# A state-space vision block on one core: side work of the scans repriced, reordered and split into other lanes

## The chip, the cores and the metric

The kernel runs on one core of a Trainium2 chip. The metric is the device time of one execution in microseconds (us). The engines of the core are PE (TensorE), DVE (VectorE), ACT (ScalarE), POOL (GpSimd) and SP (SyncE), which issues the DMAs here. Each has a queue of its own, takes its instructions in order, and waits on semaphores for the others.

## What is computed

The input is 8 images of 96 channels and 64 x 64 positions. The first layer is a group norm, a layer norm, an input projection with a depthwise 3 x 3 convolution and SiLU, a selective scan in four directions, a gated layer norm, an output projection, and a convolutional branch with Gelu and channel attention. The second layer is linear attention without softmax and a feed-forward part in quantized numbers. Cut to its core:

```python
xi = silu(conv2d(xi, conv_w, conv_b, groups=D_INNER))        # D_INNER = 192
xs = concat([x_hwwh, flip(x_hwwh, -1)], 1)                   # K = 4 directions of length L = 4096
x_dbl = einsum('bkdl,kcd->bkcl', xs, x_proj_w)
dts, Bs, Cs = split(x_dbl, ...)                              # rank 6, and 16 + 16 states
delta = softplus(einsum('bkrl,kdr->bkdl', dts, dt_w) + dt_bias)
h = exp(delta * A) * h + (delta * u) * B                     # one step; 16 states a channel
y = einsum('bkdn,bkn->bkd', h, C) + Ds * u
...
y = layer_norm(sum of the four directions) * silu(z); x1 = inp * skip_scale + out_proj(y)
cb = conv2d(gelu(conv2d(layer_norm(x1))))                    # then gated by channel attention
```

All scans together are 8 images x 4 directions x 192 channels x 16 states, each of 4096 steps.

## The kernel before

**The scans.** The images are taken in four pairs, p = 0 to 3. For each p there are four directions k, for each k four pieces of the sequence of 1024 steps (ci), and for each piece three tiles of channels (T). That makes 192 jobs. A job has four groups, a group four units, and a unit is one tile of 128 rows (32 channels of 4 states) by 1024 steps. The loop at the end of `phase_b` goes over the units two at a time; such a step is called a pair here, so a group is two pairs, and there are 768 groups. For each pair:

- ACT makes two tiles da, the decays, `exp(A * delta)`, two units ahead (`decay`; da has four buffers);
- DVE multiplies pu by bm into pb twice and runs two scans into hc (`scan`);
- POOL keeps the last column (carry) and multiplies hc by cm.

Once a group PE spreads du over the states into the PSUM tile pu (`spread`, two matmuls of 512 columns). There is one pu, so the spread for the next group can begin only when DVE has done the multiplications of the second pair, and DVE needs it for the first pair of the next group. Once a group PE also adds up the states of the group before (`total`, 16 small matmuls into half of bank yp), and ACT copies that out (y).

**The side work.** All the rest runs between the scans: the norms, taps and projections of the pair of images that comes next (`before_scans`, with `norms` and `convs`), the gate and output projection of the pair before (`gate`), everything behind it (`rest`), transposes of the scan's sum (`columns`). Each of these is a Python generator, called a lane. `Slots` holds the lanes and is run twice for each pair, once ahead of the scan and once behind the decays and, in every second pair, behind spread and total. One run is a slot; `slots.at` counts them. Four slots are a group: 1 ahead of the first scan, 2 behind the decays that follow it, 3 ahead of the second scan, 0 behind the decays, spread and total. A job has 16 slots. In a slot each lane may issue instructions up to its next `yield`. A lane that needs a PSUM bank asks `take(pe, act)` with what the work costs PE and ACT, by a price written into the code; it gets the bank when it is free and both budgets are above zero. The budgets grow by RATE in each slot, up to CAP; `pay` books more. Slot 6 and 7 of a job belong to Softplus (`steps`), which uses both banks; a `take` marked long stays away from slots 4 to 7. `after(n, f)` puts off a call by n slots.

The order that results is binding: the wrapper `InOrder` ties each instruction of an engine to the one before it, which is why nearly every instruction of the profile carries its line, L245. Nothing moves at run time; a lane's instruction at the wrong place delays all that follow on its engine.

**What has to be there in time.** A job is prepared one job ahead. If its inputs are not made yet (`while (p, k % 2, c) not in there`), 16 slots are run without a scan.

**Buffers.** Lanes share tiles u0 to u15 (`unit(i)`), each with one buffer. `norms` uses two input tiles in turn, one for the transposed rows, one for the normalized rows, two for the layer norm. `convs` copies its three results raw and runs SiLU on all three together, since SiLU and Gelu need a table other than that of exp and ln: ACT loads it ahead, and `exps()` loads the first one again behind.

Of the kernel before, what the change touches and what calls it, by code (L numbers as in the profile page):

```python
# [25 lines left out]
R = 6  # L26
G = 32
CH = 1024
# [233 lines left out]
class Slots:  # L262
# [6 lines left out]
    RATE, CAP = (1.4, 1.6), (2.2, 2.2)  # L269

    def __init__(self, *banks):
        self.lanes, self.first, self.at, self.due = [], None, 0, {}
        self.banks, self.held, self.big = banks, set(), set()
        self.left = [0.0, 0.0]
# [4 lines left out]
    def take(self, pe, act, long=False):  # L279
        while True:  # L280
            i = 1 if self.at % 2 and not long else 0

            due = long and self.at % 16 in (4, 5, 6, 7)
            if i not in self.held and not due and min(self.left) > 0:
                self.held.add(i)
                self.pay(pe, act)
                return self.banks[i]
            yield
# [14 lines left out]
    def run(self):  # L303
        self.at += 1
        self.left = [min(v + r, c) for v, r, c in zip(self.left, self.RATE, self.CAP)]
        for f in self.due.pop(self.at, ()):
            f()
        if self.first is not None and next(self.first, self) is self:
            self.first = None
        turn = self.at % len(self.lanes) if self.lanes else 0  # L310
        for lane in self.lanes[turn:] + self.lanes[:turn]:
            if next(lane, self) is self:
                self.lanes.remove(lane)

    def idle(self):
        return not (self.lanes or self.first or self.due)


def wait(n):
    for _ in range(n):  # L320
        yield


class Slots:

    RATE, CAP = (1.4, 1.6), (2.2, 2.2)

    def __init__(self, *banks):
        self.lanes, self.first, self.at, self.due = [], None, 0, {}
        self.banks, self.held, self.big = banks, set(), set()
        self.left = [0.0, 0.0]

    def pay(self, *times):
        self.left = [v - t for v, t in zip(self.left, times)]

    def take(self, pe, act, long=False):
        while True:
            i = 1 if self.at % 2 and not long else 0

            due = long and self.at % 16 in (4, 5, 6, 7)
            if i not in self.held and not due and min(self.left) > 0:
                self.held.add(i)
                self.pay(pe, act)
                return self.banks[i]
            yield  # L350

    def take_big(self, *which):

        while self.big & set(which):
            yield
        self.big |= set(which)

    def give(self, bank):
        i = self.banks.index(bank)
        self.after(1, lambda: self.held.remove(i))  # L360

    def after(self, n, f):
        self.due.setdefault(self.at + n, []).append(f)

    def run(self):
        self.at += 1
        self.left = [min(v + r, c) for v, r, c in zip(self.left, self.RATE, self.CAP)]
        for f in self.due.pop(self.at, ()):
            f()
        if self.first is not None and next(self.first, self) is self:  # L370
            self.first = None
        turn = self.at % len(self.lanes) if self.lanes else 0
        for lane in self.lanes[turn:] + self.lanes[:turn]:
            if next(lane, self) is self:
                self.lanes.remove(lane)

    def idle(self):
        return not (self.lanes or self.first or self.due)


def wait(n):
    for _ in range(n):
        yield


class Slots:

    RATE, CAP = (1.5, 1.7), (2.2, 2.2)

    def __init__(self, *banks):
        self.lanes, self.first, self.at, self.due = [], None, 0, {}
        self.banks, self.held, self.big = banks, set(), set()
        self.left = [0.0, 0.0]

    def pay(self, *times):  # L400
        self.left = [v - t for v, t in zip(self.left, times)]

    def take(self, pe, act, long=False):
        while True:
            i = 1 if self.at % 2 and not long else 0

            due = long and self.at % 16 in (4, 5, 6, 7)
            if i not in self.held and not due and min(self.left) > 0:
                self.held.add(i)
                self.pay(pe, act)  # L410
                return self.banks[i]
            yield

    def take_big(self, *which):

        while self.big & set(which):
            yield
        self.big |= set(which)

    def give(self, bank):  # L420
        i = self.banks.index(bank)
        self.after(1, lambda: self.held.remove(i))

    def after(self, n, f):
        self.due.setdefault(self.at + n, []).append(f)

    def run(self):
        self.at += 1
        self.left = [min(v + r, c) for v, r, c in zip(self.left, self.RATE, self.CAP)]
        for f in self.due.pop(self.at, ()):  # L430
            f()
        if self.first is not None and next(self.first, self) is self:
            self.first = None
        turn = self.at % len(self.lanes) if self.lanes else 0
        for lane in self.lanes[turn:] + self.lanes[:turn]:
            if next(lane, self) is self:
                self.lanes.remove(lane)

    def idle(self):
        return not (self.lanes or self.first or self.due)  # L440
# [7 lines left out]
def phase_b(  # L448
# [8 lines left out]
    with ExitStack() as ctx:  # L457
# [106 lines left out]
        def steps(job):  # L564

            p, k, ci, c, T, at = where(job)
            if T == 0:
                sts[job // 3] = gp.tile([2 * R, CH], F32, name="st")
                r0 = 64 + R * (k // 2)
                for b in range(2):  # L570
                    nc.sync.dma_start(
                        sts[job // 3][R * b : R * b + R, :],
                        xd_d[k % 2][2 * p + b][r0 : r0 + R, at],
                    )
            dtw = gp.tile([2 * R, 128], F32, name="dtw")
            nc.sync.dma_start(dtw, a["dtw"][:, k, T, :])
# [7 lines left out]
            for i, hs in enumerate(halves):  # L584
# [4 lines left out]
                pe.matmul(bank, dtw, sts[job // 3][:, hs], start=True, stop=True)  # L589
# [80 lines left out]
        def gate(p, js, ready=lambda j: None):  # L670
# [12 lines left out]
            for n, at in enumerate(ats):  # L683
                then = ats[n + 1] if n + 1 < len(ats) else None
                xc, sq = [], []
                for T in range(3):
                    bank = yield from slots.take(1.0, 1.3)
# [20 lines left out]
                for T in (2, 0, 1):  # L708
                    bank = yield from slots.take(1.0, 2.1)
# [23 lines left out]
                for b in range(2):  # L733
                    bank = yield from slots.take(1.3, 0.6)
# [11 lines left out]
        def norm(u, v):  # L746

            bank = yield from slots.take(0.45, 1.2)
# [6 lines left out]
            bank = yield from slots.take(0.45, 2.0)  # L755
# [38 lines left out]
        def squeeze(s, u, pieces):  # L794
# [4 lines left out]
            for i in pieces:  # L799
# [4 lines left out]
                bank = yield from slots.take(0.8, 0.0, True)  # L804
                for tap in range(9):
# [9 lines left out]
                    if dx == 2 and tap < 8:  # L815
                        yield
                        slots.pay(0.8, 0.0)
# [18 lines left out]
        def rest(b, s):  # L836
# [29 lines left out]
            for j in range(8):  # L866
# [3 lines left out]
                bank = yield from slots.take(0.9, 0.0, True)  # L870
                for dx in range(3):
# [7 lines left out]
                    if dx == 1:  # L879
                        yield  # L880
                        slots.pay(0.45, 0.8)
# [78 lines left out]
            def fold(t, lhsT, rhs, m):  # L960
                bank = yield from slots.take(0.2, 0.3)
# [14 lines left out]
            for j in range(8):  # L976
                v = nx
                bank = yield from slots.take(0.9, 0.7)
# [20 lines left out]
                for i in range(3):  # L999
                    bank = yield from slots.take(0.2, 1.9)  # L1000
# [8 lines left out]
                bank = yield from slots.take(0.3, 1.3)  # L1009
# [91 lines left out]
        def before_scans(p):  # L1101
# [13 lines left out]
            def project(o, b, main, mix, rows, at, t=None):  # L1115
                half = b % 2
                bank = yield from slots.take(0.9, 0.6)
# [10 lines left out]
            def norms(b):  # L1128
                def u(i):
                    return unit((6 if at_once and b % 2 else 12) + i)  # L1130
# [4 lines left out]
                def fetch(j):  # L1135
                    t = u(j % 2)[:, 0 : 4 * C].rearrange("p (g c) -> p g c", c=C)
# [8 lines left out]
                for j in js:  # L1145
                    x = nxt
                    if j < 7:
                        nxt = fetch(j + 1)
# [11 lines left out]
                    yield  # L1160
                    bank = yield from slots.take(0.1, 2.5)
# [3 lines left out]
                    inp = u(3)[0:C, 0:512]  # L1165
                    for i, q in enumerate(quarters):
                        se.activation(
                            inp[:, q], xt[:, q], AF.Square, bias=ngm[:, i : i + 1],
# [9 lines left out]
                    yield from wait(3)  # L1178
                    for i, q in enumerate(quarters):
# [24 lines left out]
            def convs(b):  # L1204
# [5 lines left out]
                def u(i):  # L1210
                    return unit(3 * half + i if at_once else 12 + i)
# [13 lines left out]
                for j in js:  # L1225
# [7 lines left out]
                    for i, w in enumerate((wz, wmain, wmix)):  # L1233
                        bank = yield from slots.take(1.3 if i else 0.45, 0.0, i > 0)
                        taps = 1 if i == 0 else 9
                        for t in range(taps):
# [8 lines left out]
                            if t in (2, 5):  # L1245
                                yield
                                slots.pay(1.3, 0.0)
# [7 lines left out]
                    z, main, mix = raw  # L1255
                    slots.pay(0.0, 4.7)
# [12 lines left out]
                    t = gp.tile([128, 512], F32, name="turn", bufs=2) if at_once else None  # L1269
                    yield from project(0, b, main, mix, slice(0, 64), ats[j], t)  # L1270
# [25 lines left out]
            there_all = set()  # L1296
            if at_once:
                for half in range(2):
                    slots.lanes.append(convs(2 * p + half))
                    if p:  # L1300
                        slots.lanes.append(norms(2 * p + half))
                while len(there_all) < 2:
                    yield
            else:
                for half in range(2):
# [713 lines left out]
```

## Time and profile before

| | before |
|---|---|
| median of 3 runs | 11310.33 us (11296.98 to 11315.09) |
| profiled execution, its time | 11307.01 us |
| span of that execution | 11305.2 us |
| busy: PE, PEld | 8037.9, 3168.4 us |
| busy: DVE | 10538.6 us, 93% |
| busy: ACT | 6622.9 us, 59% |
| busy: POOL | 9032.5 us, 80% |
| mean granted PE clock | 0.813 |
| first multiplication by bm, last scan's end | 226.5, 10966 us |

Two costly groups of instructions and the busy shares over 40 slices of the span:

```profile
L245 DVE TENSOR_TENSOR_SCAN hc<-da,carry,pb 128x1024 f32<-128x1024 f32 x2304 | 5284.5, 2341 | 97.3 <-ACT da L245 84.7
L245 DVE TENSOR_TENSOR pb<-pu,bm 128x1024 f32<-128x1024 f32 x3072 | 3612.9, 1227 | 270.3 <-PE pu L245 244.6
...
DVE 4999899999998999999999999999999999999984
```

In a group's line come the engine, the operation, what it writes and reads, the shape and the count; then the busy time of all in us and the mean of one in ns; then the idle time of the engine just ahead of them, and what ended most of it. In the slices a 9 is 90% or more of a slice of 283 us.

### The profile page before, as it was taken

The page shows a single profiled execution, that of the slowest core. Times are in us where ns is not written, and L with a number is a line of the kernel's source. Part 1 is how long each engine was busy: PE and PEld are TensorE (multiplying, and loading weights), DVE is VectorE, ACT ScalarE, POOL GpSimd, SP SyncE. Part 2 cuts the span into 40 slices and gives each one's busy share as a digit, 9 for nine tenths or more (in the row PEclk, how much of TensorE's full clock was granted, in tenths as well). Part 3 has the DMA queues.
Part 4 walks back from the last instruction along what each step waited for, and adds up shares of the span by engine and source line. Part 5 has one row for each costly group of instructions (what it writes and reads, how often), then busy time and mean ns, then how long its engine had stood idle before and what let it go on. Part 6 is the DMA issues. An engine that isn't in the chain of part 4 may idle for free.

```text
span 11305.2 us, 127593 instructions
## 1 busy us (share of the span) xinstructions
PE 8037.9 (71%) x39452; PEld 3168.4 (28%) x39452; DVE 10538.6 (93%) x6651; ACT 6622.9 (59%) x9183; POOL 9032.5 (80%) x6649
## 2 busy tenths in 40 slices
PE   7856887555568868867667876677757676665778
PEld 3312332222223323323222332233222233222223
DVE  4999899999998999999999999999999999999984
ACT  2545665444465666657766666667645656774554
POOL 2787777877897887898888778988879889997870
PEclk8877888777778878878888888788878787777889
DMA  3455444543554566665454555655644555553551
GB/s 113 144 181 164 145 154 158 174 141 129 162 186 153 165 167 190 197 204 186 154 159 154 157 172 180 198 168 169 199 148 156 163 162 189 176 170 126 175 159 37
DMA packets 893945, 1832.98 MB, mean 162 GB/s; under 512 B 244797, under 2 KB 415742, under 8 KB 886222
## 3 DMA queue, kind: packets, MB, share of 16 engines
q1 hardware_dynamic: 893262, 1824.82, 51.5%
q8 instruction: 313, 5.13, 0.2%
q14 instruction: 370, 3.03, 0.1%
HBM read 1403.95 MB, written 420.42 MB: 161 GB/s over the span
## 4 chain that ended last, share of the span: by engine, by line
PE 39%; issue 24%; DVE 16%; POOL 8%; ACT 8%; DMA 4%; SPq 0%; DVEq 0%; POOLq 0%; ACTq 0%
PE yp L245 13%; PE pu L245 13%; PE pg L245 10%; DVE hc L245 9%; DVE pb L245 5%; POOL hc L245 5%; ACT u L245 3%; ACT da L245 3%; PE t L245 2%; ACT L245 1%; POOL u L245 1%; DMA bm<-xd 1%; POOL turn L245 1%; PE ps L188 1%; DMA cm<-xd 1%
## 5 line engine op out<-in xcount | busy, mean ns | idle before, releaser
L245 POOL TENSOR_TENSOR hc<-hc,cm 128x1024 f32<-128x1024 f32 x3072 | 7231.3, 2359 | 698.3 <-DVE hc L245 467.2
L245 DVE TENSOR_TENSOR_SCAN hc<-da,carry,pb 128x1024 f32<-128x1024 f32 x2304 | 5284.5, 2341 | 97.3 <-ACT da L245 84.7
L245 PE MATMUL pu<-du,c_sel 128*128 128x512 f32 x3072 | 2438.3, 939 | 2205.5 <-DVE pb L245 2201.9
L245 DVE TENSOR_TENSOR pb<-pu,bm 128x1024 f32<-128x1024 f32 x3072 | 3612.9, 1227 | 270.3 <-PE pu L245 244.6
L245 ACT ACTIVATE da<-dl,c_alog 128x1024 f32<-128x1024 f32 x3072 | 3363.0, 1142 | 143.7 <-DVE hc L245 121.8
L245 ACT COPY y<-yp 128x256 f32<-128x256 f32 x768 | 284.9, 371 | 2657.8 <-PE yp L245 2522.8
L245 PEld LDWEIGHTS pu<-du,c_sel 128*128 128x128 f32 x3072 | 799.3, 283 | 3469.7 <-DVE pb L245 2676.7
L245 DVE TENSOR_TENSOR_SCAN hc<-da,pb 128x1024 f32<-128x1024 f32 x768 | 1715.5, 2282 | 54.8 <-ACT da L245 53.5
L245 PE MATMUL yp<-hc,c_add 128*32 128x256 f32 x24576 | 1639.3, 411 | 39.3 <-ACT dls L245 34.4
L245 PEld LDWEIGHTS yp<-hc,c_add 128*32 128x32 f32 x24576 | 761.6, 119 | 1183.5 <-issue 608.0
L245 POOL COPY carry<-hc 128x1 f32<-128x1 f32 x2304 | 424.1, 184 | 806.3 <-DVE hc L245 771.1
L245 ACT ACT_TABLE_LOAD x570 | 731.3, 1283 | 27.0 <-DMA cb<-y 16.9
L245 POOL TENSOR_TENSOR u<-u,u 96x512 f32<-96x512 f32 (+1 forms) x426 | 538.1, 1269 | 115.1 <-ACT u L245 104.3
L245 POOL TENSOR_TENSOR du<-du,dls 128x1024 f32<-128x1024 f32 x192 | 453.4, 2361 | 158.3 <-ACT dls L245 156.5
L245 ACT COPY u<-pg 128x512 f32<-128x512 f32 (+5 forms) x384 | 212.8, 554 | 501.1 <-PE pg L245 490.2
L245 ACT COPY u<-yp 96x512 f32<-96x512 f32 (+5 forms) x336 | 179.9, 536 | 427.2 <-PE yp L245 409.1
L245 PE MATMUL pg<-ain,wmain 96*128 96x512 f32 x792 | 378.2, 622 | 30.3 <-ACT u L245 25.6
L245 PE MATMUL pg<-ain,wmix 96*128 96x512 f32 x792 | 370.9, 613 | 15.4 <-ACT u L245 15.0
L245 PE MATMUL yp<-prev,ident 128*128 128x256 f32 x768 | 308.1, 492 | 10.5 <-ACT dls L245 9.0
L245 PEld LDWEIGHTS yp<-prev,ident 128*128 128x128 f32 x768 | 211.6, 277 | 340.3 <-issue 272.5
L245 PE MATMUL yp<-u,c_centres 128*128 128x512 f32 (+3 forms) x622 | 284.2, 660 | 27.0 <-ACT u L245 15.2
L245 PE MATMUL pg<-st,dtw 12*128 12x512 f32 x384 | 223.9, 663 | 45.3 <-ACT u L245 26.7
(341 smaller groups left out, 7152.8 us busy)
## 6 DMA issues: line engine op xcount, KB each, us to landing
dl<-dl SPq DMA_DIRECT2D x768, 512.0 KB
bm<-xd SPq DMA_DIRECT2D x512, 512.0 KB
cm<-xd SPq DMA_DIRECT2D x512, 512.0 KB
du<-xi SPq DMA_DIRECT2D x192, 512.0 KB
dl<-dls SPq DMA_DIRECT2D x192, 512.0 KB
ya<-y SPq DMA_DIRECT2D x384, 128.0 KB
prev<-ya SPq DMA_DIRECT2D x384, 128.0 KB
xi<-u SPq DMA_DIRECT2D x152, 256.0 KB
```

Of the source, the lines that this page charges most:

```text
L188: nc.tensor.matmul(pc.rearrange("p (h w) -> p h w", w=W), w[:, t, :], pad[:, 8 * j + dy : 8 * j + dy + 8, dx : dx + W], start=(t == 0), st ...
L245: op(*args, **kw)
```

## The change

- `Slots` stood in the file three times, each hiding the one before it; one is left. Its refill goes from (1.5, 1.7) us a slot for PE and ACT to (1.7, 1.7), its cap from 2.2 to 2.4.
- Nearly all prices of PE are about doubled; some of ACT are lowered (that of ln and exp from 2.0 or 2.1 to 1.3).
- A long `take` names its length in slots and stays away from slot 6 of a job if it would reach it.
- SiLU waits for a slot 2 of a group (`slots.at % 4`), but not slot 6 of a job. The last taps ahead of Gelu, and Gelu, wait for an even slot.
- Lanes are in two lists. `before_scans`, `norms` and `convs` stand in `later`, which is served behind `lanes`, unless `behind()` says that fewer rows than one in 35 slots are done (for p of 2 and 3).
- For p of 2 and 3, norms of both images in turn are one lane and the taps of both are another, where there was one lane for all. The taps use the tiles u16 and up.
- `norms` has one input tile, fetched for the next row behind the transposes; it squares into another tile and normalizes in place. `project` behind the taps writes into the tile of z, raw[0].
- st and dtw hold the two halves of a piece in rows 0 to 11 and 32 to 43, in half the columns, with one load for each half; the two matmuls use these rows.

```diff
-    RATE, CAP = (1.5, 1.7), (2.2, 2.2)
+    RATE, CAP = (1.7, 1.7), (2.4, 2.4)
...
-            due = long and self.at % 16 in (4, 5, 6, 7)
+            due = self.at % 16 <= 6 < self.at % 16 + long
...
-        turn = self.at % len(self.lanes) if self.lanes else 0
-        for lane in self.lanes[turn:] + self.lanes[:turn]:
-            if next(lane, self) is self:
-                self.lanes.remove(lane)
+        order = [self.lanes, self.later]
+        for lanes in order[::-1] if self.behind() else order:
+            turn = self.at % len(lanes) if lanes else 0
+            for lane in lanes[turn:] + lanes[:turn]:
+                if next(lane, self) is self:
+                    lanes.remove(lane)
...
-                pe.matmul(bank, dtw, sts[job // 3][:, hs], start=True, stop=True)
+                rows = slice(32 * i, 32 * i + 2 * R)
+                pe.matmul(bank, dtw[rows, :], sts[job // 3][rows, :], start=True, stop=True)
...
-                    bank = yield from slots.take(1.0, 2.1)
+                    bank = yield from slots.take(1.8, 1.3)
                     minus_mean(bank, sq, T)
...
-            bank = yield from slots.take(0.45, 1.2)
+            bank = yield from slots.take(0.9, 1.2)
             pe.matmul(bank[0:C, :], centre, v, start=True, stop=True)
...
                     if dx == 2 and tap < 8:
                         yield
-                        slots.pay(0.8, 0.0)
+                        while tap == 5 and slots.at % 2:
+                            yield
+                        slots.pay(1.2, 0.0)
...
-                        bank = yield from slots.take(1.3 if i else 0.45, 0.0, i > 0)
+                        bank = yield from slots.take(2.6 if i else 0.9, 0.0, 3 if i else 0)
...
-                                slots.pay(1.3, 0.0)
+                                slots.pay(2.6, 0.0)
...
+                    while slots.at % 4 != 2 or slots.at % 16 == 6:
+                        yield
                     slots.pay(0.0, 4.7)
                     se.activation(main, main, AF.Silu, bias=convb[:, 0:1])
...
-                    t = gp.tile([128, 512], F32, name="turn", bufs=2) if at_once else None
-                    yield from project(0, b, main, mix, slice(0, 64), ats[j], t)
+                    yield from project(0, b, main, mix, slice(0, 64), ats[j], u(0)[:, 0:512])
...
-                for half in range(2):
-                    yield from norms(2 * p + half)
-                    yield from convs(2 * p + half)
+                begun = slots.at
+                slots.behind = lambda: slots.at - begun > 35 * len(rows_done)
+                def both(f):
+                    yield from f(2 * p)
+                    yield from f(2 * p + 1)
+                slots.later += [both(norms), both(convs)]
```

## The prediction

> **What bounds the kernel now.** First the slices of the page: DVE is at 9 tenths or more nearly everywhere. So I cut the span by the stages of the side work (stretches in us; then length, busy time and count of each engine, granted PE clock, DMA share, GB/s):
>
> ```profile
> core 0: us, PE busy (x) PEld busy (x) DVE busy (x) ACT busy (x) POOL busy (x), PEclk, DMA share, GB/s
> 1063.00:1917.00 854.00, 697.22 (x3030) 283.84 (x3033) 769.91 (x456) 537.07 (x883) 613.78 (x449) 0.86 0.48 150
> 1917.00:2980.00 1063.00, 572.06 (x3092) 223.74 (x3088) 1061.70 (x634) 455.31 (x491) 849.53 (x605) 0.73 0.45 147
> 2980.00:3982.00 1002.00, 740.23 (x3361) 275.76 (x3354) 916.20 (x544) 613.57 (x947) 855.07 (x657) 0.83 0.54 172
> 4364.00:5256.00 892.00, 693.63 (x3136) 271.05 (x3138) 834.59 (x500) 547.88 (x728) 788.23 (x633) 0.82 0.62 200
> 5713.00:7070.00 1357.00, 1046.91 (x5310) 404.38 (x5304) 1292.62 (x771) 885.95 (x1340) 1120.37 (x808) 0.84 0.55 165
> 7070.00:7983.00 913.00, 673.09 (x3179) 270.27 (x3171) 861.56 (x513) 618.94 (x872) 805.41 (x645) 0.81 0.56 182
> ```
>
> Where side work is thin (1917 to 2980) DVE idles 1.3 us of 1063: the scans alone set the pace, 6.7 us a pair, 13.47 us a group of two pairs. Where norms and taps run, DVE idles 84 (854 - 770), 86, 57, 64 and 51 us. Over the loop (227 to 10966) the same subtraction gives 411 us. That is all this change can win; the 227 us ahead of the loop and the 339 us behind it are untouched. The waits of DVE say who takes it:
>
> ```profile
> engine line waited for: us in total, times, longest us
> DVE pb L245 <- PE pu L245: 244.6, 113, 11.0
> DVE hc L245 <- ACT da L245: 138.3, 91, 5.4
> DVE pb L245 <- DMA bm<-xd: 23.6, 13, 6.1
> ```
>
> PE is late with pu, or ACT with a decay. One instance of each, from the timeline (start, duration, engine):
>
> ```profile
> 3495.72 2.03 PE L245 MATMUL yp<-u,c_centres 128*128 128x512 f32 x6
> 3497.68 5.42 PE L245 MATMUL pg<-ain,wmain 96*128 96x512 f32 x12
> 3503.03 2.08 PE L245 MATMUL yp<-u,c_centres 64*64 64x512 f32 x8
> 3505.05 2.84 PE L245 MATMUL pg<-ain,wmain 96*128 96x512 f32 x6
> 3507.72 1.88 PE L245 MATMUL pu<-du,c_sel 128*128 128x512 f32 x4
> 3509.64 2.36 DVE L245 TENSOR_TENSOR pb<-pu,bm 128x1024 f32<-128x1024 f32 x2 [3.73 <-PE pu L245]
> ...
> 1752.06 1.28 ACT L245 ACT_TABLE_LOAD   x1
> 1753.35 1.34 ACT L245 ACTIVATE u<-u,convb 128x512 f32<-128x512 f32 x2
> 1754.60 0.61 ACT L245 ACTIVATE u<-u 128x512 f32<-128x512 f32 x1
> 1755.23 1.28 ACT L245 ACT_TABLE_LOAD   x1
> ```
>
> (An f32 matmul stands there as two records.) Nine taps and a layer norm are queued ahead of the spread, whose pu comes 3.7 us late. Three taps take 2.6 to 2.8 us, and the old price was 1.3. A SiLU batch is 1.28 + 1.34 + 0.61 + 1.28 = 4.5 us. In that instance a c_vec activation and a second table switch with Softplus follow it, and the scan waits 5.36 us.
>
> **Part by part.**
>
> *Prices and rate.* No instruction is removed: the built programs have the same 20,206 matmuls, 39452 records in the trace. Only their places move. Old refill 1.5 PE-us a slot against 1.3 for three taps: 0.87 slot. New: 2.6/1.7 = 1.53 slots. A group has 13.47 us, of which spread (1.9) and total (1.93 in the same timeline) take 3.8; the 9.6 left hold 11 matmuls of 512 columns at 0.87. I counted, in the order of the two built programs, the side matmuls between successive spreads in units of 512 columns, and put the pu waits of the trace beside them:
>
> | units | groups before | wait, us | mean | groups after | at the same mean |
> |---|---|---|---|---|---|
> | under 6 | 539 | 58 | 0.1 | 523 | 59 |
> | 6 to 8 | 84 | 33 | 0.39 | 107 | 42 |
> | 8 to 11.5 | 97 | 59 | 0.61 | 133 | 81 |
> | over 11.5 | 47 | 85.5 | 1.82 | 4 | 7 |
>
> Sum 235 to 189: **-46**. It is conservative: the middle rows' means come from busy stages. By stage: the norms and taps of p = 1 go from 7.1 units a group over 57 groups (90 us of excess over the floor) to about 5.4 over 78; the stages 4364 to 5256 and 5713 to 7983, at 4.6 to 6 units, lost 0.8 to 1.0 us a group; the gate alone (8415 to 8866, 5.3 units) 0.26. Between these, 0.5 to 0.65 us for a well spaced stage, taken through the stages with taps, the whole comes to **-165** with ACT's share in it.
>
> *SiLU behind decays alone, Gelu likewise.* ACT's segments between pairs of decays: SiLU or Gelu batches with 5.2 us or more of work are 29 before (53 us of waits, 1.8 each) and 15 after; those with the copy of y, which waits for PE, go from 33 to 9. At unchanged means all ACT waits go from 134 to 118: **-16**; if the SiLU ones nearly vanish, -50. A pair leaves 6.7 - 2.19 (two decays) = 4.5 us: a batch just fits. Here a rule of the Trainium skill is against it: "ScalarE: Activation LUTs", What ACT_TABLE_LOAD costs, adds some 1.38 us of drain to each load. By it a batch takes 7.3 us, 2.8 too many for 83 batches, +230 us. The row decides: 1752.06 + 1.28 = 1753.34, and the next instruction starts at 1753.35. No drain; I take 4.5.
>
> *Lists and pace.* Side work of the next p (later) stands behind the rest, except where rows are under one per 35 slots. In the built program no stage misses its due point (the loop of 16 slots without a scan is never entered), and stages end where they did (p = 2 at group 569 for 563; p = 1's taps at 137 for 116, before thin stretches). Cost 0. If the cover went, each entry is 16 slots, about 54 us.
>
> *Norms and taps as two lanes for p of 2 and 3.* Same instructions; more lanes to fill slots. 0, in the counts already.
>
> *st and dtw in two row groups.* +128 and +192 DMAs on SP at 0.32 us an issue: 102 us of a queue that often waits on others. du's load stands up to three issues (1 us) later and is used over five slots (17 us) later. 0; if not covered, 320 x 0.32 = 102 us.
>
> *Norms with one input buffer.* fetch(j+1) moves behind the transposes of j; SP stands until PE has made them, and dl, bm and cm queue behind. 48 rows (8 in each of 6 images). SP already waits for DVE and POOL on nearly every group; between 0 and 2 us a row (a slot is 3.4), I take 0: up to +96.
>
> *The projection written over z.* ACT's copy must now wait until z's store has landed, in 56 rows, where another buffer served. Nearest row: ACT's copies of 256 KB loads (turn<-xi) wait 48 us in 15 cases, 3.2 each. Behind ACT stand y's copy and the next decays, behind these the scan. Between 0 and 3.2 x 56 = 180; most projections come a pair later and ACT has slack (537 busy of 854), so +10.
>
> *The clock.* "TensorE: Matmul & The Clock Gate", Part 1, says that PE drops to half clock after an idle window of about 3.4 us. It speaks against thinning PE. The row: granted clock 0.86 at 7 units a group, 0.82 at 5.6, 0.73 where thin, and a spread takes 3.78 us where thin against 1.98. By the rule at its worst every tap doubles: 5.4 x 1.73 + 7.6 is 17 us a group, +3.5 over some 400 groups, +1400. But PE would then never be idle, so the rule itself releases the clock. By the rows 0.86 to 0.82 costs 5% of 9 us, inside the slack. 0, and the upper half of my range.
>
> **Sum.** Same-class means -62, stage densities -165; the middle, -115, with +10 gives -105 to -155. I take -125: 11,307 - 125 = **11,182**, from the profiled execution (11,307.0; span 11,305.2), 3 us under the median of the runs, which I neglect.
>
> **Rivals.**
> 1. *Nearly all tap and SiLU waits go* (18%). For it: the gate alone shows 0.26 us a group at like load. Against: many pu waits have PE itself waiting for ACT in a norm ("yp<-u,c_centre", up to 11.5 us), and such chains stay. 411 down to 160: about 11,055.
> 2. *The waits only change place* (8%): mid-sized groups rise from 181 to 240, and if they take 1 us more each with lower clock and ACT chains, -62 + 59: about 11,304, no change.
> 3. *Slower: z's store in ACT's queue* (8%). 56 rows x 3.2 us, plus 48 x 2 from the fetch behind the transposes: 179 + 96 - 125 = +150: 11,457. It decides from 2.2 us a row of DVE time lost in 56 rows. Against: ACT has several us of slack in a pair.
> Forecast case: 66%.
>
> **How the numbers follow.** Measured differences under 0.2% (23 us) cannot be told from none. Faster takes the forecast and rival 1: 0.84. Same 0.08, slower 0.08. The range holds the forecast's own ends (-62 plus 40 of unknown costs to -165 and a bit), most of rival 1 and the near part of rival 2: 11,045 to 11,290.
>
> **What would show it.** Right: DVE waits on pu fall to about 160 and on decays to about 90; groups over 14 us grow rare in the taps of p = 0 and 1; no ACT batch with SiLU is followed by a scan wait over 2 us. PE busy and DVE busy stay, clock within 0.02. Wrong: xd copies on ACT released by DMA with sums over 50 us; bm or dl waits on DVE over 60; clock near 0.77; or pu waits still over 220 with their weight on c_centre behind ACT.

## The result and the profile after

The changed kernel takes 11170.24 us (median of 4 runs, 11167.43 to 11173.18) against 11311.11 us before (median of 4 runs); the ratio is 0.9878, interval 0.9861 to 0.9895. The profiled execution has a span of 11171.2 us. 134 us are gone from the span; the loop is 139 us shorter and the part behind it 4 us longer (in the trace of before the last scan ends at 10968.9, not at 10966). The first view of the kernel after is that of DVE's waits (engine, what it waited for; us in all, times, longest):

```profile
engine line waited for: us in total, times, longest us
DVE pb L245 <- PE pu L245: 170.2, 76, 12.3
...
DVE hc L245 <- ACT da L245: 89.2, 63, 7.9
...
DVE pb L245 <- DMA bm<-xd: 14.9, 9, 3.4
```

DVE's waits for PE's pu fell by 74 us and those for ACT's decays by 49. The second view cuts both kernels by p, from the first multiplication of each p to that of the next. First the kernel before, then the kernel after (length, busy times with counts, granted PE clock, DMA share, GB/s):

```profile
226.50:2926.70 2700.20, 1786.00 (x8558) 703.95 (x8558) 2582.81 (x1536) 1385.26 (x1857) 2079.40 (x1520) 0.79 0.48 154
2926.70:5659.90 2733.20, 2021.27 (x9893) 792.46 (x9893) 2585.00 (x1539) 1737.57 (x2496) 2338.85 (x1753) 0.82 0.57 178
5659.90:8361.90 2702.00, 2002.29 (x9899) 792.30 (x9898) 2584.57 (x1539) 1723.70 (x2473) 2270.23 (x1681) 0.82 0.55 171
8361.90:10968.90 2607.00, 1779.38 (x9452) 686.86 (x9450) 2578.59 (x1539) 1577.54 (x2019) 2274.50 (x1646) 0.80 0.52 163
```

```profile
227.10:2832.70 2605.60, 1742.37 (x8558) 690.06 (x8558) 2578.10 (x1536) 1376.85 (x1854) 2081.12 (x1520) 0.80 0.50 160
2832.70:5542.60 2709.90, 1987.35 (x9893) 780.66 (x9893) 2585.00 (x1540) 1733.48 (x2496) 2338.99 (x1753) 0.83 0.58 179
5542.60:8228.70 2686.10, 1988.28 (x9897) 783.02 (x9896) 2581.21 (x1540) 1718.55 (x2472) 2271.03 (x1681) 0.83 0.55 172
8228.70:10830.80 2602.10, 1771.89 (x9453) 682.17 (x9451) 2578.47 (x1539) 1574.46 (x2019) 2275.07 (x1646) 0.80 0.52 164
```

DVE's busy time is the same to a few us in every row, so each row's length is its floor of some 2580 us plus idle. The gains are 95, 23, 16 and 5 us. In p = 0, where neither gate nor rest runs yet beside taps and norms, 117 us of idle fell to 28. In p = 1 and 2, where they do, most of it stayed (148 to 125, 117 to 105). That is uneven, though p = 1 and 2 hold more side work. The granted clock rose by 0.01 or stayed.

A new wait appears on ACT. In the list of its waits in the kernel after:

```profile
ACT u L245 <- DMA xd<-u: 71.4, 15, 12.7
...
ACT u L245 <- DMA zs<-u: 55.0, 12, 10.5
```

The same list before:

```profile
ACT u L245 <- DMA zs<-u: 4.8, 2, 3.2
...
ACT u L245 <- DMA xd<-u: 2.2, 1, 2.2
```

One place in the timeline of the kernel after shows what that does to a scan (start, duration, engine, instruction; in brackets idle ahead of it and its releaser):

```profile
7237.76 1.13 SPq L647 DMA_DIRECT2D zs<-u  x2
...
7242.83 0.58 ACT L245 COPY u<-pg 76x512 f32<-76x512 f32 x1 [7.38 <-DMA zs<-u]
7243.44 0.27 SPq L647 DMA_DIRECT2D xd<-u  x1
...
7248.73 0.59 ACT L245 COPY u<-yp 128x512 f32<-128x512 f32 x1 [5.32 <-DMA xd<-u]
7249.21 2.19 ACT L245 ACTIVATE da<-dl,c_alog 128x1024 f32<-128x1024 f32 x2
...
7250.45 4.59 DVE L245 TENSOR_TENSOR_SCAN hc<-da,carry,pb 128x1024 f32<-128x1024 f32 x2 [7.89 <-ACT da L245]
```

The projection's copy over z waits until z's store has landed, 5.1 us behind the first of the two issues shown. The next row's z is copied over the projection, and waits for the projection's store in the same way. The decays queue behind both, and the scan is 7.9 us late.

### The profile page after: what moved, and what is told of

It is laid out like the page before. It is cut to its first block, busy times and chain, and to the rows that moved or that the text cites. A ratio compares the mean times of both kernels' runs of the same rounds, so it can differ in the third digit from the quotient of the medians.

```text
span 11171.2 us, 128095 instructions
## 1 busy us (share of the span) xinstructions
PE 7943.3 (71%) x39452; PEld 3134.6 (28%) x39452; DVE 10531.6 (94%) x6651; ACT 6601.8 (59%) x9179; POOL 9035.0 (81%) x6649
## 4 chain that ended last, share of the span: by engine, by line
PE 22%; issue 15%; DVE 10%; POOL 5%; ACT 4%; DMA 3%; SPq 0%; DVEq 0%; POOLq 0%; ACTq 0%
PE pu L245 8%; PE yp L245 8%; DVE hc L245 6%; PE pg L245 4%; DVE pb L245 4%; POOL hc L245 3%; ACT u L245 2%; PE t L245 2%; ACT da L245 1%; POOL u L245 1%; DMA bm<-xd 1%; DMA xd<-u 1%; POOL turn L245 0%; ACT w_dt.float L245 0%; ACT L245 0%
## 5 line engine op out<-in xcount | busy, mean ns | idle before, releaser
L245 POOL TENSOR_TENSOR hc<-hc,cm 128x1024 f32<-128x1024 f32 x3072 | 7233.6, 2360 | 623.3 <-DVE hc L245 403.1
L245 DVE TENSOR_TENSOR_SCAN hc<-da,carry,pb 128x1024 f32<-128x1024 f32 x2304 | 5269.1, 2327 | 77.0 <-ACT da L245 64.3
L245 PE MATMUL pu<-du,c_sel 128*128 128x512 f32 x3072 | 2415.6, 931 | 2237.1 <-DVE pb L245 2232.7
L245 DVE TENSOR_TENSOR pb<-pu,bm 128x1024 f32<-128x1024 f32 x3072 | 3590.8, 1213 | 185.9 <-PE pu L245 170.2
L245 ACT ACTIVATE da<-dl,c_alog 128x1024 f32<-128x1024 f32 x3072 | 3356.0, 1140 | 117.5 <-DVE hc L245 101.1
L245 ACT COPY y<-yp 128x256 f32<-128x256 f32 x768 | 284.7, 371 | 2622.2 <-PE yp L245 2493.3
L245 PEld LDWEIGHTS pu<-du,c_sel 128*128 128x128 f32 x3072 | 787.9, 279 | 3485.9 <-DVE pb L245 2715.8
L245 DVE TENSOR_TENSOR_SCAN hc<-da,pb 128x1024 f32<-128x1024 f32 x768 | 1709.9, 2267 | 27.9 <-ACT da L245 25.0
L245 PE MATMUL yp<-hc,c_add 128*32 128x256 f32 x24576 | 1637.0, 411 | 27.5 <-ACT u L245 9.7
L245 PEld LDWEIGHTS yp<-hc,c_add 128*32 128x32 f32 x24576 | 761.5, 119 | 1175.8 <-issue 595.9
L245 POOL COPY carry<-hc 128x1 f32<-128x1 f32 x2304 | 426.4, 185 | 785.1 <-DVE hc L245 743.3
L245 POOL TENSOR_TENSOR u<-u,u 96x512 f32<-96x512 f32 (+1 forms) x426 | 538.3, 1270 | 98.5 <-ACT u L245 89.6
L245 ACT COPY u<-pg 128x512 f32<-128x512 f32 (+5 forms) x406 | 225.6, 556 | 633.2 <-PE pg L245 581.5
L245 POOL TENSOR_TENSOR du<-du,dls 128x1024 f32<-128x1024 f32 x192 | 453.6, 2362 | 131.6 <-ACT dls L245 128.9
L245 PE MATMUL pg<-ain,wmain 96*128 96x512 f32 x792 | 392.2, 646 | 44.3 <-ACT u L245 40.3
L245 ACT COPY u<-yp 96x512 f32<-96x512 f32 (+5 forms) x338 | 180.7, 535 | 399.3 <-PE yp L245 304.3
L245 PE MATMUL pg<-ain,wmix 96*128 96x512 f32 x792 | 376.1, 624 | 23.0 <-ACT u L245 20.2
L245 PE MATMUL yp<-prev,ident 128*128 128x256 f32 x768 | 316.3, 504 | 29.8 <-ACT dls L245 16.2
L245 PEld LDWEIGHTS yp<-prev,ident 128*128 128x128 f32 x768 | 211.7, 279 | 363.3 <-issue 258.6
L245 PE MATMUL yp<-st,dtw 12*128 12x512 f32 x384 | 234.3, 692 | 36.0 <-ACT u L245 24.4
L245 PE MATMUL pg<-st,dtw 12*128 12x512 f32 x384 | 222.6, 660 | 45.4 <-ACT u L245 25.8
```

The lines of the kernel that those rows point to most:

```text
L245: op(*args, **kw)
```

## The experiments

Each ran beside the kernel before on the same chip; ratios are to that. Several chips served; the kernel before has a median of 11305 to 11311 us on them, so the medians of two experiments can differ by some 6 us through the chip alone. "Theory" in the expectations stands for the explanation under test.

**1. A buffer of its own for the projection.**

```diff
-                    yield from project(0, b, main, mix, slice(0, 64), ats[j], u(0)[:, 0:512])
+                    yield from project(
+                        0, b, main, mix, slice(0, 64), ats[j], gp.tile([128, 512], F32, name="turn", bufs=2)
+                    )
```

> The changed kernel, but the projection behind the taps writes into the tile turn (two buffers) and not over z, so ACT's copy need not wait for z's store; the places of all instructions stay. Theory A (the waits of ACT for stores, 55 us for zs and 71 us for xd in the profile after, lengthen the scans in p = 1 and 2): those waits vanish and the time falls by 40 to 80 us, to about 11,110. Theory B (ACT has slack for them, only the rare one of 7 us or more reaches a scan): 0 to 25 us, to about 11,155.

11122.12 us, ratio 0.9838 (0.9825 to 0.9852): 48 us faster than the changed kernel. Of ACT's 27 waits for zs and xd (126 us in all) three are left, 9 us, and p = 2 gains most (2652 for 2686 us). DVE's waits in its profile:

```profile
DVE pb L245 <- PE pu L245: 147.9, 73, 9.9
...
DVE hc L245 <- ACT da L245: 80.5, 54, 10.4
...
DVE pb L245 <- DMA bm<-xd: 12.9, 6, 3.9
```

Theory A holds, at the lower part of its size. Of DVE's waits those on pu fell by 22 us and those on decays by 9, so of what these two show, most reached DVE by PE. That ACT's late copies hold the PSUM banks of PE's next taps, with spread behind them, is the likely way; it was not shown by itself.

The buffer is not wholly its own: `columns` uses `turn` as well, and stores from it. The same fault is left in two places of p = 1, and DVE's two longest waits for decays (9.7 and 10.4 us) follow them. The second:

```profile
3172.27 0.58 ACT L245 COPY turn<-pg 76x512 f32<-76x512 f32 x1 [13.90 <-DMA y<-turn]
...
3175.01 2.35 DVE L245 TENSOR_TENSOR_SCAN hc<-da,carry,pb 128x1024 f32<-128x1024 f32 x1 [10.37 <-ACT da L245]
```

**2. One lane for norms and taps of p = 2 and 3 again.**

```diff
-                slots.later += [both(norms), both(convs)]
+                def serial():
+                    for half in range(2):
+                        yield from norms(2 * p + half)
+                        yield from convs(2 * p + half)
+                slots.later.append(serial())
```

> The changed kernel with norms and taps of p = 2 and 3 in one lane again, one image after the other, all else kept. Theory A (two lanes fill the slots more evenly and are worth time): slower by 30 to 60 us, about 11,215. Theory B (they make taps of one image and norms of the other meet in the same group, and PE waits for ACT in both): faster by 20 to 60 us, about 11,130. In the built order no group has over 11.5 units of side matmuls (4 in the changed kernel).

11209.65 us (0.9918, 0.9904 to 0.9931), 39 us slower than the changed kernel. But ACT waited 210 us for zs and xd here, so the two causes are mixed. Hence a second run, with both edits:

> Norms and taps of p = 2 and 3 in one lane again, together with the buffer of its own for the projection. With one lane alone ACT waited 210 us for stores of zs and xd, against 126 with two. If one lane was slower by 39 us only because the projection over z comes sooner there: within 20 us of the own buffer with two lanes, 11,122. If two lanes are worth time by themselves: 30 to 60 us slower, about 11,165.

11154.29 us (0.9859, 0.9844 to 0.9873), 32 us over the run with its own buffer and two lanes; the two intervals overlap by 0.0008. The two lanes are worth some 30 us beside the rest of the change, as far as that can be told. DVE's waits for pu are 18 us longer than in experiment 1 (165.9 for 147.9), and those for bm 21 us:

```profile
DVE pb L245 <- DMA bm<-xd: 33.6, 21, 3.9
```

**3. The prices and refill of before, all else changed.**

```diff
-    RATE, CAP = (1.7, 1.7), (2.4, 2.4)
+    RATE, CAP = (1.5, 1.7), (2.2, 2.2)
...
-                        bank = yield from slots.take(2.6 if i else 0.9, 0.0, 3 if i else 0)
+                        bank = yield from slots.take(1.3 if i else 0.45, 0.0, 3 if i else 0)
```

(and likewise every other price, ACT's too)

> The changed kernel with the prices, refill and cap of before. In the built order 43 groups have over 11.5 units of side matmuls, as before (47), against 4. If the prices carry the gain by PE's waits for pu: these rise to 220 or more from 170, and the time by 60 to 100 us, to about 11,250. If the gain comes from the gates of SiLU and the lanes: under 30 us, about 11,190.

11320.08 us (1.0012, 1.0006 to 1.0019): the whole gain is gone. Both waits return to the level of the kernel before, ACT's too, though both gates are in place:

```profile
DVE pb L245 <- PE pu L245: 255.9, 99, 9.9
...
DVE hc L245 <- ACT da L245: 131.6, 86, 11.5
```

**4. No gates for SiLU and Gelu.**

```diff
-                    while slots.at % 4 != 2 or slots.at % 16 == 6:
-                        yield
...
-                        while tap == 5 and slots.at % 2:
-                            yield
```

> The changed kernel without the two gates: SiLU may stand in any slot, the last taps and Gelu too. In the built order 43 batches of SiLU or Gelu share their stretch between decays with the copy of y, against 9. If the gates carry the gain in ACT's waits: waits on da rise from 89 to 110 to 135 us, the time by 25 to 50 us, to about 11,205. If the prices alone did that: within 15 us of 11,170.

11177.76 us (0.9887, 0.9873 to 0.9900), no difference from the changed kernel that the intervals show. DVE's waits in its profile:

```profile
DVE pb L245 <- PE pu L245: 160.4, 72, 11.2
...
DVE hc L245 <- ACT da L245: 98.2, 66, 6.8
```

Batches that share their stretch with the copy of y went from 9 to 43. Waits for decays are 9 us longer, those for pu 10 us shorter, and the time shows no cost.

**5. Which price.** First the new price for the taps of `convs` and the new refill alone, all other prices as before:

> The changed kernel with the prices of before for everything but the taps of convs (2.6 for three) and the refill (1.7, cap 2.4), which stay new. Theory A (the taps' price is what carries the gain): p = 0, where convs and norms alone run, keeps its 2606 us and the whole is within 30 us of 11,170. Theory B (the prices of gate, norms and rest matter as much, since p = 1 and 2 hold most of the side work): 60 to 100 us slower, about 11,250. In the built order 12 groups have over 11.5 units of side matmuls, against 4 and, with all old prices, 43.

11174.57 us (0.9877, 0.9862 to 0.9892), the same as the changed kernel, with 2611 us for p = 0. Then the complement: all prices new, but the taps' as before.

```diff
-                        bank = yield from slots.take(2.6 if i else 0.9, 0.0, 3 if i else 0)
+                        bank = yield from slots.take(1.3 if i else 0.45, 0.0, 3 if i else 0)
...
-                                slots.pay(2.6, 0.0)
+                                slots.pay(1.3, 0.0)
```

> The complement of the run with new tap prices alone: all prices new, only three taps of convs at 1.3 again (0.45 for z's single tap). In the built order 47 groups have over 11.5 units, as many as in the kernel before. If the taps' price carries the gain: p = 0 takes 2660 us or more again (2606 in the changed kernel), the whole 90 to 150 us more than the changed kernel, about 11,290. If any one set of prices would do: under 40 us more.

11284.65 us (0.9981, 0.9972 to 0.9989): of 141 us 114 are lost, 71 of the profiled execution's in p = 0 (2676 us). So one number, the cost of three taps, carries nearly all of the gain, and the other prices nearly nothing.

**6. That number in the kernel before**, and nothing else of the change:

```diff
-                        bank = yield from slots.take(1.3 if i else 0.45, 0.0, i > 0)
+                        bank = yield from slots.take(2.6 if i else 0.9, 0.0, i > 0)
...
-                                slots.pay(1.3, 0.0)
+                                slots.pay(2.6, 0.0)
```

> The kernel before with the taps' price alone changed (2.6 for three, 0.9 for z), in two lines; refill 1.5, one list, no gates, no pace. 10 groups have over 11.5 units. If the price needs nothing else of the change: p = 0 falls from 2700 to about 2610 us and the whole to about 11,180. If it needs the lists and the pace, because lanes are late: p = 1 and 2 rise and take the gain back, 11,280 or more.

11110.03 us (0.9828, 0.9813 to 0.9843), 60 us faster than the changed kernel. DVE's waits in its profile:

```profile
DVE pb L245 <- PE pu L245: 149.3, 66, 10.6
...
DVE hc L245 <- ACT da L245: 55.4, 56, 4.0
```

Both are below those after. The expectation that lanes would be late without lists and pace did not come true: DVE's longest wait in the loop is 10.6 us, where a stage that misses its point holds it over 80 (experiment 7). The p rows are 2614, 2666, 2652 and 2611 us. The own buffer with the taps' price alone comes to the same:

> A candidate for the fastest: a buffer of its own for the projection, new prices for the taps alone. If the other prices do nothing: within 15 us of 11,122. If they matter once the waits for stores are gone: 20 to 40 us more.

11121.85 us (0.9840, 0.9825 to 0.9854). Its interval and that of the two lines overlap; the two-line kernel is the fastest measured, and all the rest of the change with the buffer mended, in experiment 1 with all new prices and here without, adds nothing to it that these runs show.

It has one lane for norms and taps, as the second run of experiment 2 has, and that run is 44 us slower (the intervals, 0.9844 to 0.9873 and 0.9813 to 0.9843, just do not meet; 33 us of it in p = 1, 22 in p = 2). So with one lane something else of the change costs time, and the two lanes win most of it back. What it is was not found; DVE's waits for bm are 33.6 us there and 18.1 in the two-line kernel.

**7. No pace.**

```diff
-                slots.behind = lambda: slots.at - begun > 35 * len(rows_done)
```

> The changed kernel without the pace: lanes of the next p always stand behind the rest. In the built order the loop of 16 slots without a scan is entered ten times. At 16 slots of 3.36 us each entry would cost up to 54 us, +540 us, if the side work fills them; if a slot without a scan takes only as long as the little work in it (the transposes on POOL, 1.3 us a slot), about 20 us each, +200 us, about 11,370.

11349.18 us (1.0032, 1.0021 to 1.0043), 179 us over the changed kernel. In the list of waits of its profile:

```profile
DVE hc L245 <- ACT da L245: 257.4, 71, 94.4
```

Two of these waits hold 94.4 and 83.1 us, one at the end of p = 1 and one at the end of p = 2: ten turns of 16 slots without a scan, some 18 us each. With all prices raised and the next images' lanes set behind all others, those lanes are late, and the pace is what mends it. It mends a need that the change itself made: the two-line kernel has neither lists nor pace, and no such wait.

**8. A smaller refill** (1.5 for PE) with the own buffer:

> The buffer of its own for the projection, and PE's refill at 1.5 in place of 1.7, with the new prices. If thinner PE work is still better: 10 to 40 us faster than 11,122. If the pu waits left are PE waiting for ACT in the norms and not PE's load, nothing: within 20 us. If the lanes run late and crowd at the end: slower.

11131.22 us (0.9839, 0.9823 to 0.9856), the same as 1.7. DVE's waits in its profile:

```profile
DVE pb L245 <- PE pu L245: 132.7, 62, 9.7
...
DVE hc L245 <- ACT da L245: 68.4, 40, 8.6
...
DVE pb L245 <- DMA bm<-xd: 32.7, 21, 4.6
```

Against experiment 1 the waits for pu and decays are 27 us shorter, and those for bm 20 us longer. So thinner work on PE still shortens its own waits here, and nearly as much comes back at another place; why bm comes later was not tried.

## Why the prediction was right, and where its terms were not

The forecast was 11,182 us; the measured median is 12 us below it, and -141 us stands against -125. Point by point:

- *The bound.* Right: DVE's busy time did not move, head and tail hardly (+1 and +4 us), and the loop gave all of it. DVE's waits were forecast at about 160 and 90 us and are 170.2 and 89.2. The clock, forecast within 0.02, is 0.820 for 0.813.
- *Prices and rate.* Right in kind. The term was put between -46 at unchanged means and -165 by stage densities. Taken out of the changed kernel, the taps' price is worth 114 us (experiment 5) and all prices 150 (experiment 3); put alone into the kernel before, it is worth 197 (experiment 6), more than either figure. The stage argument was the better one, and where it was firmest, the norms and taps of p = 1, it was still too low: that stage fills the stretch below of the kernel after, and DVE idles 19 us of it (1068 - 1049), where 84 us stood before and 39 to 50 were foreseen (78 groups at 0.5 to 0.65 us).

```profile
1026.00:2094.00 1068.00, 809.85 (x3825) 328.28 (x3828) 1049.22 (x625) 661.34 (x1057) 838.24 (x609) 0.83 0.49 153
```

- *SiLU and Gelu behind decays.* Mis-sized. It was put at -16 to -50 us; taken out of the changed kernel, the gates are worth 7, which is within the noise. DVE's waits for decays did fall as foreseen, but by the prices: experiment 3 has both gates and 131.6 us, experiment 6 has none, nor a new price of ACT, and 55.4. That the long batches came from raw taps that PE delivered late, and not from SiLU's place, is the likely reading; it was not shown by itself.
- *The projection written over z.* The largest error of a single term: +10 us was taken, out of 0 to 180; it is 48. The row taken as nearest, 3.2 us a wait, was a prefetched load; the waits are 4.6 us in the mean for z's store and 4.8 for the projection's. Here a store is issued when the copy is about to start, and lands 5.1 us later in the instance shown. That most projections come later was true (12 waits for z's store in 56 rows) and did not save the others; and the waits of the next z for the projection's store (15) were not thought of.
- *Two lanes.* Taken at 0; experiment 2 puts it at some 30 us in favour of the change, as a cover for a cost that the rest of the change brings (experiment 6).
- *Lists and pace.* No stage misses its point, as foreseen (DVE's longest wait in the loop is 12.3 us); the lists were not undone alone. The cost without cover was put at 54 us an entry and is 18: slots without a scan hold little work (in the 94 us of the first wait ACT copies 16 projections and does nothing else until the next decays).
- *The clock.* The rule of the Trainium skill on idle windows ("TensorE: Matmul & The Clock Gate", Part 1) did not turn against the change. In the stage that was thinned, the norms and taps of p = 1, the grant did fall, from 0.86 to 0.83 (0.82 was foreseen), and the stage idled less all the same. Over p = 0 as a whole it is 0.80 for 0.79.
- *The table loads.* 566 loads (line L245) after for 570 before. In the trace before, 556 of 579 loads are followed by the next instruction within 0.05 us; so it does not show the drain that "ScalarE: Activation LUTs", What ACT_TABLE_LOAD costs, adds to each.
- *st and dtw, and the single input of norms.* Put at 0 and not tried alone. The waits for bm fell (14.9 for 23.6 us), so with two lanes SP's longer queue did no visible harm. With one lane they are 34 us in both runs of experiment 2. Whether that is the fetch behind the transposes, the added loads of st and dtw or something else stays open.
- *The signs.* Those named for right came. Groups over 14 us in the stretch of p = 0 fall from 45 to 12 of 192; and of 56 batches with SiLU none is followed by a scan that waits over 2 us for ACT, where 11 were before (both counted in the traces). One sign named for wrong came too: ACT's copies of the projection that waited for a store sum to 55 us, over the 50 named. It marked a real cost, smaller than the gain.

That the sum came so close is in part luck. The price was worth more than foreseen, and the costs, the buffer's 48 us above all, were larger too; the errors cancel to a part. Nor was -125 the outcome of the sum: it was chosen between -105 and -155. And in the table 523 groups at the first row's mean (58 us over 539 groups) are 56 us, not 59, which makes that sum -49.

## What to carry to other kernels

A planner that doles out work by prices is only as good as its dearest price: measure the piece that is issued most often, and put that number right, before gates, orders and paces are built around a wrong one. When a buffer is saved by writing over one that is being stored, the wait for that store stands in the queue of the engine that writes, ahead of everything else there; look for it among the waits for DMAs. Undo the parts of a change one by one even if it won: here two lines of it were faster than all of it.

## What had not been expected of the hardware

A store of z, 256 KB, held the tile 5.1 us from its issue to the start of ACT's copy in the instance shown, in a stretch (p = 2) with DMA engines busy 55% of the time; waits of ACT for the stores of z and of the projection reached 10.5 and 12.7 us. And spreading PE's work out cost little clock: with the norms and taps of p = 1 over 78 groups for 57, PE's busy share of that stage fell from 82% to 76% and the grant from 0.86 to 0.83.
